# Cross attention in a decoder layer: exponentials of two head groups added on VectorE, masked weights on GpSimd, scans moved

## The chip, the cores and the metric

The kernel runs on one core of a Trainium2 chip. The metric is the device time of one execution in microseconds (us). A core has engines that each work through their own queue of instructions in order: TensorE (PE, matrix products; PEld is its weight load), VectorE (DVE), ScalarE (ACT), GpSimd (POOL) and SyncE (SP, which issues most DMAs). Engines wait for one another through semaphores. SBUF is the working memory of 128 partitions; PSUM is the memory that TensorE writes to, and GpSimd does not read it here.

## The reference

Three blocks on x of shape (4, 512, 512): causal self attention, causal cross attention over a context, and a feed-forward block with two experts' weights. All are float32. The cross attention, cut to what matters:

```python
def _mha(q, k, v):                       # q = layernorm(x), k = v = ctx; 16 heads of 32
    scores = jnp.einsum('bhqd,bhkd->bhqk', qh, kh) / math.sqrt(hd)
    causal = ki <= qi
    scores = jnp.where(causal[None, None], scores, -10000.0)
    attn = jax.nn.softmax(scores, axis=-1)
    return jnp.einsum('bhqk,bhkd->bhqd', attn, vh)

x = x + self_attention(layernorm(x))     # causal, mask of -inf, with projections
x = x + _mha(layernorm(x), ctx, ctx)
x = x + feed_forward(layernorm(x))
```

The mask of the cross attention is -10000 and not minus infinity, so a row whose largest score lies very low would give weight to the keys behind it as well. The kernel computes that weight: for each query the sum of the later context rows ("behind", a running sum from the end) and their number, both times exp(-10000 - maximum).

## The kernel before

The four batches run one after the other in the loop at L845. Each passes through these stages: maxima of the self scores (`with_maxima` L781, filled up with projection matmuls of other blocks), self attention (`attend` L811), output projection (L632), maxima of the cross scores, cross attention, transposes and layernorm (`add_cross` L662), and the feed-forward matmuls, most of which are used as filler in later maxima stages. The order on PE, DVE, ACT and POOL is written out by hand (`manual_schedule`, L836): an engine's queue holds its instructions in the order in which the Python code issues them. Buffers and PSUM come from pools. PSUM has four pairs of banks (`pair`, L65); a new pair waits for the readers of the one that it replaces.

Heads go in four groups g of four heads (128 partitions). The keys go in four blocks of 128; the attention works in units (g, (0,)), (g, (1,)) and (g, (2, 3)). For one unit, `scores` (L360) multiplies keys and queries for four heads and adds minus the row maximum, in two PSUM pairs of two heads each; ScalarE takes the exponential (L402) and GpSimd clears what lies above the diagonal (`affine_select`, L404). Two units later `values` (L416) multiplies the exponentials with the values and, in a second set of matmuls with a matrix of ones, adds them up for the denominators (the loop over u, L425). After a group's last unit `divide` (L493) adds the masked weights, inverts the denominators through two 32x32 block transposes (`inverse`, L481) and multiplies.

In the self attention groups 0 to 2 are "added" (L265): the ones matmuls are left out; instead `add_up` (L453) adds the exponentials of the later units onto the first unit's tile on VectorE, and one set of four matmuls with ones (`summed`, L462) is done on the sum while the next group runs. In the cross attention no group is added.

In the cross attention `behind` (L618) computes the running sum of a group of context columns on VectorE, called in `attend` at L829 after the scores of the group's first unit. `masked` (L348), called after the scores of the group's last unit, spreads the row maxima with one matmul, takes the exponential on ScalarE (L353), and makes two products with `min` on VectorE (L356 and L357), for the numerator and for the denominator.

`with_maxima` also takes a list `norms` of small jobs, one of which it puts behind every second unit's reductions; the cross call at L863 gives none. In `out_projection` the matmuls of L638 come first, with transposes of the context as side work, and then the additions to x and the layernorm.

Of the kernel before, what the change touches and what calls it, by code (L numbers as in the profile page):

```python
# [9 lines left out]
F32 = mybir.dt.float32  # L10
# [16 lines left out]
def decoder_layer(  # L27
# [232 lines left out]
    class Attention:  # L260
        def __init__(self, q_t, k_t, v, cross, name):
            self.q_t, self.k_t, self.v, self.cross, self.name = q_t, k_t, v, cross, name
            self.nm, self.mrow, self.pv, self.out = {}, {}, {}, None
            self.more, self.sums, self.rden, self.e = {}, {}, {}, None
            self.added = () if cross else range(NC - 1)  # L265

        def maxima(self, g, blocks):

# [79 lines left out]
        def masked(self, g):  # L348

            bc = pair(f"mb_{self.name}_{g}")  # L350
            nc.tensor.matmul(bc[:, 0, :], lhsT=same, rhs=self.mrow[g], start=True, stop=True)
            count = work.tile([P, S], F32, tag="count", name=f"ct_{self.name}_{g}")
            nc.scalar.activation(count, bc[:, 0, :], AF.Exp, bias=mbias)  # L353

            beh = self.e.beh_t[:, g, :]
            nc.vector.scalar_tensor_tensor(beh, count, 1.0, beh, ALU.min, ALU.mult)  # L356
            nc.vector.scalar_tensor_tensor(count, count, 1.0, cnt, ALU.min, ALU.mult)  # L357
            self.more[g] = (beh, count)

        def scores(self, g, blocks):  # L360


            at = {j: sum(S - k * P for k in blocks if k < j) for j in blocks}
            N = sum(S - j * P for j in blocks)
            name = f"{self.name}_{g}_{blocks[0]}"
            scs = [pair(f"sc_{name}_{n}") for n in range(2)]
            for j in blocks:
                for r in range(HG):
                    h = slice(r * HD, (r + 1) * HD)
                    nc.tensor.matmul(  # L370
                        scs[r // 2][:, r % 2, at[j] : at[j] + S - j * P],
                        lhsT=self.k_t[h, g, j * P : (j + 1) * P],
                        rhs=self.q_t[h, g, j * P :],
                        start=(j == blocks[0]),
                        stop=False,
                        skip_group_check=(len(blocks) > 1),
                    )
# [12 lines left out]
            if blocks[0] == 0 and g in self.added:  # L390

                self.sums[g] = act.tile(
                    [P, 2, 2, S], F32, tag=("ck_t", "beh_t")[g % 2], name=f"sum_{name}"
                )
            for n in range(2):

                W = N if len(blocks) == 1 else S
                if blocks[0] == 0 and g in self.added:
                    pt = self.sums[g][:, n]
                else:  # L400
                    pt = work.tile([P, 2, W], F32, tag=f"pt{blocks[0]}", name=f"pt_{name}_{n}")
# [12 lines left out]
            return pts  # L414

        def values(self, g, blocks, pts):  # L416

            first, last = blocks[0] == 0, blocks[-1] == NT - 1  # L420
            if first:
                self.pv[g] = pair(f"pv_{self.name}_{g}")
            pv = self.pv[g]
            at = {j: sum(S - k * P for k in blocks if k < j) for j in blocks}
            for u in range(1 if g in self.added else 2):  # L425
                for j in blocks:
                    for r in range(HG):
                        h = g * HG + r
                        nc.tensor.matmul(  # L429
                            pv[r * HD : (r + 1) * HD, u, j * P :],  # L430
                            lhsT=ones if u else self.v[:, j, h * HD : (h + 1) * HD],
                            rhs=pts[r // 2][:, r % 2, at[j] : at[j] + S - j * P],
                            start=(j == 0),
                            stop=(j == NT - 1),
                        )
            if first and g == 0 and not self.cross:
                self.out = act.tile([P, NC, S], F32, tag="o_t", name=f"oT_{self.name}")
            if first and g - 1 in self.added:
                self.sum_in = pv if g in self.added else pair(f"ls_{self.name}")
                self.summed(g - 1, self.sum_in)  # L440
            if first and g - 2 in self.added:
                self.scale(g - 2)
            if blocks == (1,) and g - 1 in self.added and g not in self.added:
                self.spread(g - 1, self.sum_in)
                self.scale(g - 1)
            if last and g in self.added:
                nc.scalar.copy(self.out[:, g, :], pv[:, 0, :])
                if g > 0:
                    self.spread(g - 1, pv)
            elif last:  # L450
                self.divide(g)
# [38 lines left out]
            )  # L490
            return den_t

        def divide(self, g):  # L493
            pv = self.pv.pop(g)
            num, den = pv[:, 0, :], pv[:, 1, :]
            if self.cross:
                beh, count = self.more.pop(g)
                nc.vector.tensor_tensor(count, den, count, ALU.add)
                nc.vector.tensor_tensor(beh, num, beh, ALU.add)
                num, den = beh, count  # L500
                self.out = self.e.beh_t
            rden = self.inverse(g, den)
            nc.vector.tensor_tensor(self.out[:, g, :], num, rden, ALU.mult)
# [128 lines left out]
    def out_projection(e, a, sides):  # L632

        b = e.b
        pms = [pair(f"pm_o{b}_{n}") for n in range(2)]
        for c in range(NC):
            for t in range(NT):
                nc.tensor.matmul(  # L638
                    pms[t // 2][:, t % 2, :],
                    lhsT=a.out[:, c, t * P : (t + 1) * P],  # L640
                    rhs=wo_sb[:, c, :],
                    start=(c == 0),
                    stop=(c == NC - 1),
                )
            if c < NC - 1:
                run(sides[c::3])

        def add(t):
            xi = e.x[:, t, :]
            nc.vector.tensor_tensor(xi, pms[t // 2][:, t % 2, :], xi, ALU.add)  # L650

        made, norms = layernorms(lambda t: e.x[:, t, :], f"q{b}", add)
        run(norms)
        return made
# [156 lines left out]
    def attend(a, late):  # L811

        units = [(g, j) for g in range(NC) for j in ((0,), (1,), (2, 3))]
        waiting = []

        def values():
            g, j, pts = waiting.pop(0)
            a.values(g, j, pts)
            if g in a.added and j != (2, 3):
                a.add_up(*waiting[0])  # L820

        for n, (g, j) in enumerate(units):
            waiting.append((g, j, a.scores(g, j)))
            if n == 4:
                for copy in a.rows(late):
                    copy(nc.scalar.copy)
            if len(waiting) > 2:
                values()
            if a.cross and j == (0,):  # L829
                behind(a.e, g)  # L830
            if a.cross and j == (2, 3):
                a.masked(g)
        while waiting:
            values()

    with tc.manual_schedule(engines=BY_HAND):  # L836
# [8 lines left out]
        for b in range(B):  # L845
# [14 lines left out]
            norm_cross(e, made)  # L860
            ca = Attention(e.cq_t, e.ck_t, e.cv, True, f"c{b}")
            ca.e = e
            late = with_maxima(steps[3:], ca)  # L863
            if b + 2 < B:
                after.x = load_x(b + 1)
            attend(ca, late)
# [70 lines left out]
```

## Time and profile before

| | |
|---|---|
| median of 3 runs | 830.17 us (830.14 to 830.20) |
| profiled execution | 829.93 us |
| its span (first to last instruction) | 828.2 us |
| granted TensorE clock | 0.999 |
| PE / DVE / ACT / POOL busy in the span | 813.8 / 547.0 / 397.9 / 297.8 us |
| output projection, batch 1 | 287.8 to 314 us |
| maxima of the cross scores, batch 1 | 318 to 367 us |
| first cross value matmul to next projection, batch 1 | 367.06 to 397.43 us |
| the same in batches 0, 2 and 3 | 163.81, 557.0 and 732.0 us on |

How to read it: the page gives the busy time of each engine, its share of the span and the number of instructions. The chain that ended last is followed back from the last instruction, at each step to what released it, and its shares say which engine's work set the end. A timeline row is start, duration, engine, source line, operation, output<-inputs, the size of the tile and the number of instructions merged; idle time in front of it stands in brackets with what ended it. In a row of groups the two numbers after the bar are the total busy time and the mean ns of one instruction. A windows row is a stretch with its length and the busy time of PE, PEld, DVE, ACT and POOL in it, and the count of instructions in brackets.

Some durations of single instructions of before that the working uses, from the groups: L356 694 ns, L357 706 ns, L623 (the scan) 1227 ns, L498 692 ns, L499 681 ns, L484 702 ns, L486 254 ns, L487 712 ns, L503 794 ns, L402 814 ns (768 wide) and 1021 ns (1024 wide), L539 (GpSimd, two inputs, 512 wide) 1270 ns. In the timelines a GpSimd select of 256 takes 0.41 us and of 512 0.64 us where nothing holds it up; VectorE's additions of 512 and 256 take 0.68 and 0.51 us.

### The profile page before, as it was taken

To read this page: it belongs to the slowest core of one execution; us is meant where nothing else is said; L and a number is where in the kernel's file an instruction comes from. 1 tells how busy PE (TensorE), PEld (TensorE's weight loads), DVE (VectorE), ACT (ScalarE), POOL (GpSimd) and SP (SyncE) were. 2 spreads that over 40 slices of the span, in tenths; PEclk is the share of its full clock that TensorE was granted. 3 is DMA by queue.
4 is the path that set the end of the run, shared out by engine and by line. 5 is a ranking of instruction groups with operands and counts; after the bars stand their busy time and mean duration, and the time that the engine had idled before them with its cause. 6 is when DMAs were issued, how large, how long until landed. Compare 5 with 4: busy or idle time off the path is not lost.

```text
span 828.2 us, 14453 instructions
## 1 busy us (share of the span) xinstructions
PE 813.8 (98%) x5800; PEld 369.4 (45%) x5800; DVE 547.0 (66%) x937; ACT 397.9 (48%) x502; POOL 297.8 (36%) x549
## 2 busy tenths in 40 slices
PE   9999999999999999999999999999998999999998
PEld 7344444345444454334534444434543444444443
DVE  2578736877678834687858863687779835887511
ACT  2456526761546515556054651676166714574110
POOL 4434512442334732234233471244233643333100
PEclk9999999999999999999999999999999999999999
DMA  9600000001010000030100000000102000000101
GB/s 340 232 27 15 1 1 1 2 2 51 5 35 13 2 1 1 0 103 2 51 14 13 2 2 0 1 2 2 53 16 72 18 1 0 1 2 2 51 0 51
DMA packets 13539, 24.54 MB, mean 30 GB/s; under 512 B 1952, under 2 KB 1952, under 8 KB 13472
## 3 DMA queue, kind: packets, MB, share of 16 engines
q1 hardware_dynamic: 13184, 23.09, 8.2%
q8 instruction: 45, 0.74, 0.4%
q10 hardware_dynamic: 288, 0.52, 0.2%
q14 instruction: 22, 0.18, 0.1%
HBM read 19.42 MB, written 4.19 MB: 29 GB/s over the span
## 4 chain that ended last, share of the span: by engine, by line
PE 92%; ACT 3%; DVE 3%; issue 2%; DMA 0%; POOL 0%; ACTq 0%
PE pm_qk L233 12%; PE pv_c L429 9%; PE pm_u L233 7%; PE pm_d L221 7%; PE pm_v L221 7%; PE pm_o L638 7%; PE pm_e L221 6%; PE pv_s L429 6%; PE sm_c L280 6%; PE sc_s L370 5%; PE sc_c L370 5%; PE sm_s L280 5%; PE sc_s L381 1%; DVE nm_s L310 1%; PE sc_c L381 1%
## 5 line engine op out<-in xcount | busy, mean ns | idle before, releaser
L310 DVE TENSOR_REDUCE nm_c<-s_c 128x2 f32<-128x256 f32 (+3 forms) x128 | 96.3, 810 | 36.6 <-POOL s_c L298 36.6
L310 DVE TENSOR_REDUCE nm_s<-s_s 128x2 f32<-128x256 f32 (+3 forms) x128 | 96.6, 810 | 28.1 <-POOL s_s L298 28.1
L292 ACT COPY s_s<-sm_s 128x768 f32<-128x768 f32 (+1 forms) x96 | 78.9, 874 | 67.2 <-PE sm_s L280 50.9
L292 ACT COPY s_c<-sm_c 128x768 f32<-128x768 f32 (+1 forms) x96 | 78.9, 875 | 48.8 <-PE sm_c L280 34.5
L402 ACT ACTIVATE pt_c<-sc_c 128x768 f32<-128x768 f32 (+1 forms) x96 | 78.6, 883 | 28.7 <-PE sc_c L381 24.8
L298 POOL TENSOR_SCALAR_AFFINE_SELECT s_c<-s_c 128x256 f32<-128x256 f32 (+1 forms) x96 | 46.7, 487 | 119.1 <-ACT s_c L292 118.1
L404 POOL TENSOR_SCALAR_AFFINE_SELECT pt_c<-pt_c 128x256 f32<-128x256 f32 (+1 forms) x96 | 56.7, 598 | 71.0 <-ACT pt_c L402 70.1
L298 POOL TENSOR_SCALAR_AFFINE_SELECT s_s<-s_s 128x256 f32<-128x256 f32 (+1 forms) x96 | 46.9, 491 | 96.7 <-ACT s_s L292 95.7
L458 DVE TENSOR_TENSOR sum_s<-sum_s,pt_s 128x512 f32<-128x512 f32 (+1 forms) x72 | 63.2, 915 | 7.4 <-PE pv_s L429 6.4
L221 PE MATMUL pm_d<-wdown_sb,hT 128*128 128x512 f32 x128 | 60.4, 607 | 0.0
L402 ACT ACTIVATE pt_s<-sc_s 128x768 f32<-128x768 f32 (+1 forms) x72 | 55.9, 838 | 8.9 <-PE sc_s L381 6.4
L221 PE MATMUL pm_e<-wexp_sb,fT 128*128 128x512 f32 x128 | 60.2, 605 | 0.0
L233 PE MATMUL pm_u<-fT,wup_sb 128*128 128x512 f32 x128 | 59.9, 608 | 0.0
L370 PE MATMUL sc_s<-qT,kT 32*128 32x128 f32 (+3 forms) x512 | 58.2, 467 | 0.9 <-ACT sum_s L402 0.9
L233 PE MATMUL pm_qk<-xnT,wk_sb 128*128 128x512 f32 x120 | 58.6, 610 | 0.0
L638 PE MATMUL pm_o<-wo_sb,oT_s 128*128 128x512 f32 x128 | 57.8, 596 | 0.0
L221 PE MATMUL pm_v<-wv_sb,xnT 128*128 128x512 f32 x128 | 57.6, 598 | 0.0
L233 PE MATMUL pm_qk<-xnT,wq_sb 128*128 128x512 f32 x120 | 57.4, 604 | 0.0
L404 POOL TENSOR_SCALAR_AFFINE_SELECT pt_s<-pt_s 128x256 f32<-128x256 f32 (+1 forms) x72 | 48.7, 681 | 21.0 <-ACT pt_s L402 19.8
L370 PE MATMUL sc_c<-cqT,ckT 32*128 32x128 f32 (+3 forms) x512 | 51.8, 467 | 0.9 <-ACT pt_c L402 0.9
L280 PE MATMUL sm_c<-ckT,cqT 32*128 32x512 f32 (+3 forms) x512 | 49.1, 467 | 1.2 <-ACT cqT L257 1.2
L280 PE MATMUL sm_s<-kT,qT 32*128 32x512 f32 (+3 forms) x512 | 48.1, 467 | 0.0
(148 smaller groups left out, 1186.2 us busy)
## 6 DMA issues: line engine op xcount, KB each, us to landing
cv<-in_ctx_dram SPq DMA_DIRECT2D x16, 256.0 KB, 4.1
out_dram<-x SPq DMA_DIRECT2D x16, 256.0 KB, 2.0
x<-in_x_dram SPq DMA_DIRECT2D x14, 256.0 KB, 4.7
xin<-in_x_dram SPq DMA_DIRECT2D x12, 256.0 KB, 2.7
wq_sb<-in_wq_dram SPq DMA_DIRECT2D x2, 512.0 KB, 6.0
wk_sb<-in_wk_dram SPq DMA_DIRECT2D x2, 512.0 KB, 7.7
wv_sb<-in_wv_dram SPq DMA_DIRECT2D x1, 1024.0 KB, 8.3
wo_sb<-in_wo_dram SPq DMA_DIRECT2D x1, 1024.0 KB, 9.9
```

What stands on the lines that cost most here:

```text
L221: nc.tensor.matmul(pm, lhsT=lhs_t[:, c, t * P : (t + 1) * P], rhs=w[:, c, :], start=(c == 0), stop=(c == NC - 1),)
L233: nc.tensor.matmul(pm, lhsT=w[:, c, f * P : (f + 1) * P], rhs=rhs_t[:, c, :], start=(c == 0), stop=(c == NC - 1),)
L280: nc.tensor.matmul(scs[r // 2][:, r % 2, at[i] : at[i] + (i + 1) * P], lhsT=self.q_t[h, g, i * P : (i + 1) * P], rhs=self.k_t[h, g, : (i + ...
L292: nc.scalar.copy(s[:, :, :N], scs[n][:, :, :N])
L298: nc.gpsimd.affine_select(out=diagonal, in_=diagonal, compare_op=ALU.is_ge, fill=NEG, base=0, pattern=[[0, 2 * len(blocks)], [-1, P]], cha ...
L310: nc.vector.tensor_reduce(self.nm[g][:, i, 2 * n : 2 * n + 2], made[n][:, :, at[i] : at[i] + (i + 1) * P], axis=AX.X, op=ALU.max, negate=True,
L370: nc.tensor.matmul(scs[r // 2][:, r % 2, at[j] : at[j] + S - j * P], lhsT=self.k_t[h, g, j * P : (j + 1) * P], rhs=self.q_t[h, g, j * P :] ...
L402: nc.scalar.activation(pt[:, :, :N], scs[n][:, :, :N], AF.Exp)
L404: nc.gpsimd.affine_select(out=diagonal, in_=diagonal, compare_op=ALU.is_ge, fill=0.0, base=0, pattern=[[0, 2 * len(blocks)], [1, P]], chan ...
L429: nc.tensor.matmul(pv[r * HD : (r + 1) * HD, u, j * P :], lhsT=ones if u else self.v[:, j, h * HD : (h + 1) * HD], rhs=pts[r // 2][:, r % ...
L458: nc.vector.tensor_tensor(to, to, pts[n][:, :, at[j] : at[j] + S - j * P], ALU.add)
L638: nc.tensor.matmul(pms[t // 2][:, t % 2, :], lhsT=a.out[:, c, t * P : (t + 1) * P], rhs=wo_sb[:, c, :], start=(c == 0), stop=(c == NC - 1),)
```

## The change

Groups 0 and 2 of the cross attention are added: VectorE adds their exponentials into one tile, which lies in the buffer of the self values (tag `v`), and four matmuls with ones sum it during the next group, in a PSUM pair of its own (`ls`). The division of such a group comes after the next group's second unit; its numerator is taken out of PSUM right after its last unit (`gather`). The two products of `masked` go to GpSimd and lose their `min`; the last column, which has no key behind it, is set to zero by a memset instead. The scans of groups 0 and 1 go into the output projection, in front of the additions to x, and those of groups 2 and 3 between the maxima, behind the reductions of units (0, (0, 1)) and (0, (3,)).

```diff
-            self.added = () if cross else range(NC - 1)
+            self.added = (0, 2) if cross else range(NC - 1)
...
-            nc.scalar.activation(count, bc[:, 0, :], AF.Exp, bias=mbias)
-
+            nc.scalar.activation(count[:, : S - 1], bc[:, 0, : S - 1], AF.Exp, bias=mbias)
+            nc.gpsimd.memset(count[:, S - 1 :], 0.0)
             beh = self.e.beh_t[:, g, :]
-            nc.vector.scalar_tensor_tensor(beh, count, 1.0, beh, ALU.min, ALU.mult)
-            nc.vector.scalar_tensor_tensor(count, count, 1.0, cnt, ALU.min, ALU.mult)
+            nc.gpsimd.tensor_tensor(beh, count, beh, ALU.mult)
+            nc.gpsimd.tensor_tensor(count, count, cnt, ALU.mult)
...
-                self.sums[g] = act.tile(
-                    [P, 2, 2, S], F32, tag=("ck_t", "beh_t")[g % 2], name=f"sum_{name}"
-                )
+                tag = "v" if self.cross else ("ck_t", "beh_t")[g % 2]
+                self.sums[g] = act.tile([P, 2, 2, S], F32, tag=tag, name=f"sum_{name}")
...
-            if first and g - 2 in self.added:
+            if first and g - 2 in self.added and not self.cross:
                 self.scale(g - 2)
             if blocks == (1,) and g - 1 in self.added and g not in self.added:
-                self.spread(g - 1, self.sum_in)
-                self.scale(g - 1)
-            if last and g in self.added:
+                if self.cross:
+                    self.divide(g - 1, self.sum_in[:, 1, :])
+                else:
+                    self.spread(g - 1, self.sum_in)
+                    self.scale(g - 1)
+            if last and g in self.added and self.cross:
+                self.gather(g)
+            elif last and g in self.added:
...
+        def gather(self, g):
+
+            num = self.pv.pop(g)[:, 0, :]
+            beh = self.more[g][0]
+            nc.vector.tensor_tensor(beh, num, beh, ALU.add)
+
+        def divide(self, g, den=None):
+            if den is None:
+                pv = self.pv[g]
+                num, den = pv[:, 0, :], pv[:, 1, :]
             if self.cross:
-                beh, count = self.more.pop(g)
+                num, count = self.more[g]
                 nc.vector.tensor_tensor(count, den, count, ALU.add)
-                nc.vector.tensor_tensor(beh, num, beh, ALU.add)
-                num, den = beh, count
+                if g not in self.added:
+                    self.gather(g)
+                den = count
                 self.out = self.e.beh_t
...
             if c < NC - 1:
                 run(sides[c::3])
+        for g in (0, 1):
+            behind(e, g)
...
-            if a.cross and j == (0,):
-                behind(a.e, g)
...
-            late = with_maxima(steps[3:], ca)
+            scans = [(lambda g=g: behind(e, g)) for g in (2, 3)]
+            late = with_maxima(steps[3:], ca, norms=scans)
```

More of the change, by code (lines that the diff above doesn't have):

```diff
@@ L491, in inverse @@
             return den_t
-        def divide(self, g):
-            pv = self.pv.pop(g)
-            num, den = pv[:, 0, :], pv[:, 1, :]
+        def gather(self, g):
[6 more added lines that the diff above has]
+                num, den = pv[:, 0, :], pv[:, 1, :]
             if self.cross:
-                beh, count = self.more.pop(g)
+                num, count = self.more[g]
                 nc.vector.tensor_tensor(count, den, count, ALU.add)
-                nc.vector.tensor_tensor(beh, num, beh, ALU.add)
-                num, den = beh, count
+                if g not in self.added:
+                    self.gather(g)
+                den = count
                 self.out = self.e.beh_t
```

## The prediction

> **What bounds the kernel now.** Read first: the page's busy shares and its chain, then the cross-attention stage of batch 1 by itself, then the timeline inside it, then the self-attention stage of the same batch, which already adds up exponentials on VectorE.
>
> ```profile
> PE 813.8 (98%) x5800; PEld 369.4 (45%) x5800; DVE 547.0 (66%) x937; ACT 397.9 (48%) x502; POOL 297.8 (36%) x549
> PE 92%; ACT 3%; DVE 3%; issue 2%; DMA 0%; POOL 0%; ACTq 0%
> ...
> 367.06:397.43 30.37, 30.37 (x413) 12.74 (x409) 23.69 (x36) 19.86 (x26) 12.97 (x25) 1.00 0.11 36
> ```
>
> TensorE is busy all the time and is 92% of the chain; in the cross stage (last line: first value matmul to the next projection) it never idles. So work taken off TensorE there is worth its full time, until another engine's result comes too late. The other engines have room: VectorE 6.7 of 30.37, GpSimd 17.4.
>
> ```profile
> 367.06 1.06 PE L429 MATMUL pv_c<-pt_c,cv 128*32 128x512 f32 x8
> 367.94 1.04 PE L429 MATMUL pv_c<-pt_c,ones 128*32 128x512 f32 x8
> 368.92 0.39 PE L351 MATMUL mb_c<-mrow_c,same 128*128 128x512 bf16 x1
> 370.52 0.85 PE L429 MATMUL pv_c<-pt_c,cv 128*32 128x384 f32 x8
> 371.95 0.93 PE L370 MATMUL sc_c<-cqT,ckT 32*128 32x384 f32 x8
> 373.30 0.86 PE L429 MATMUL pv_c<-pt_c,cv 128*32 128x256 f32 x16
> 374.74 0.94 PE L370 MATMUL sc_c<-cqT,ckT 32*128 32x256 f32 x16
> ...
> 261.10 1.06 PE L429 MATMUL pv_s<-sum_s,v 128*32 128x512 f32 x8
> 262.10 1.22 PE L370 MATMUL sc_s<-qT,kT 32*128 32x512 f32 x8
> 263.47 0.85 PE L429 MATMUL pv_s<-pt_s,v 128*32 128x384 f32 x8
> 264.25 1.22 PE L370 MATMUL sc_s<-qT,kT 32*128 32x384 f32 x8
> 265.89 0.86 PE L429 MATMUL pv_s<-pt_s,v 128*32 128x256 f32 x16
> 266.68 1.12 PE L370 MATMUL sc_s<-qT,kT 32*128 32x256 f32 x12
> 284.20 1.04 PE L464 MATMUL ls_s<-sum_s,ones 128*32 128x512 f32 x8
> 285.06 0.83 PE L429 MATMUL pv_s<-pt_s,v 128*32 128x384 f32 x8
> ```
>
> Starts are the clean measure. With the ones matmuls (cross) the three value units of a group take 368.92-367.06 = 1.86, 1.43 and 1.44; without them (self) 1.00, 0.78 and 0.79. The summing matmuls take 0.86.
>
> ```profile
> 277.59 1.98 POOL L479 TENSOR_TENSOR oT_s<-oT_s,dt_s 128x512 f32<-128x512 f32 x1
> 278.36 2.03 DVE L458 TENSOR_TENSOR sum_s<-sum_s,pt_s 128x768 f32<-128x768 f32 x1
> 284.84 1.28 POOL L479 TENSOR_TENSOR oT_s<-oT_s,dt_s 128x512 f32<-128x512 f32 x1
> ```
>
> These decide the forecast. GpSimd's product takes 1.28 alone. Started at 277.59, while VectorE was in the addition before, it lasted to 279.57; the next addition, begun at 278.36, ended at 280.39, only 0.82 behind it. The two do not share: an addition of two SBUF tensors and a GpSimd product run one after the other, and each holds the other up for its full length.
>
> **The change part by part.** The sum goes against the profiled execution's 829.93 (span 828.2 and 1.7 around it); the median of the runs is 830.17, 0.03% above.
>
> *Ones matmuls, groups 0 and 2.* Gone 0.86 + 0.65 + 0.65 = 2.16 a group, added 0.86 for the summing matmuls: -1.30 a group, eight groups, -10.4 on the path.
>
> *Score units that now come early.* TensorE reaches a score unit sooner, but its second pair of heads needs a PSUM pair that ScalarE's exponentials free; those take 1.94 a unit of four 512-wide heads and 1.51 otherwise, as before. The self stage shows it: its score unit at 264.25 is followed by the next step (265.57) after 1.32, the cross unit at 371.95 after 1.02. In the changed program's order the summing result takes a PSUM pair too (`ls`), so that scores (2,0) wait for VectorE's denominator addition (0.69). Taken: 0.33 + 0.31 + 0.11 + 0.40 in group 0's round, 0.37 for `ls`, 0.31 + 0.31 + 0.09 in group 2's: 2.23 a batch, +8.9. Bounds: 1.5 a batch (self loses 0.8 in its first round and 0.37 in each of two more) and 3.2 (eight waits of the largest, 0.4).
>
> *VectorE.* An added group gets six additions, 2 x (0.82 + 0.68 + 0.51) = 4.0 (the six of L458 in self took 4.99 to 5.99 with GpSimd beside them); every group loses two masked products (0.69 + 0.69, L356 and L357) and a scan (1.22). The gather addition of an added group waits for GpSimd's product and for the last value matmul; behind it in VectorE's queue stand only divisions, but the summing matmuls wait for it. In the stage: +8.0 - 5.5 - 4.9, so its load hardly moves, but the additions stand behind the division of the group before, which takes 3.8 (0.69, 0.68, 0.70, 0.25, 0.71, 0.70 and gaps).
>
> *GpSimd.* Each group gets a memset (0.10) and two products of 1.28 on top of its selects (four of 0.41, two of 0.64 alone): 2.9 becomes 5.6. In its queue the products stand between the selects of unit (g,(2,3)) and those of (g+1,(0)), which TensorE's value matmuls wait for. Bounds of a product: 1.28 alone, 1.98 beside an addition; I take 1.28 and put the waits in separately.
>
> A page speaks against this part. The Trainium skill, GPSIMD Engine Reference, section 3.1 Elementwise, gives 4497 ns for a 2048-wide two-input addition, about twice VectorE's. Scaled to 512 that is an estimate of 1.12; the trace's 1.28 decides, and by the page's figure the time would come out 2.6 lower (0.16 x 4 x 4: of a batch's eight products about four stand in the way).
>
> *The turns, batch 1, from the rows above* (us from the stage's first value matmul; unit (g,j) is head group and key block):
>
> ```
> TensorE reaches     before  after   what held it in between
> values (0,0)          0.00   0.00
> values (1,0)          8.71   8.31   banks; 0.60 for the select of (1,0), behind both products
> summing group 0         -   10.60   0.55 for the gather addition behind the six additions
> values (1,1)         12.17  13.54   0.37, ls bank
> values (2,0)         17.09  18.46
> values (2,1)         20.55  21.37   0.31
> values (3,0)         25.46  26.96   0.31, 0.21; 1.45 for the second select of (3,0)
> summing group 2         -   30.11   1.40 for the gather addition
> next projection      30.37  34.27
> ```
>
> Group 0's round: the products can start at 2.55, after the spread maxima's exponential; with the first two additions between them they end at 6.59, the selects of (1,0) at 7.55 and 8.40 (TensorE wants the second at 7.86), the additions, one select after each, at 9.91 and gather at 10.53 (TensorE is there at 10.05). The worst place, group 2: the division of group 1 ends at 21.59. Then in turns: product 22.86, addition 23.69, product 24.88, addition 25.71, select 26.04, addition 26.70, select 27.05 (the one awaited, TensorE was there at 25.51), addition 27.55, select 27.90, addition 28.56, select 28.91, addition 29.41, gather 30.04 (TensorE was there at 28.70). TensorE's lost turns are 0.60 + 0.55 + 1.45 + 1.40 + 0.1 = 4.1 a batch. Behind it comes group 3's division, which waits for GpSimd's last product and ends 0.1 after the transposes want it.
>
> With the first two parts: -2.6 + 2.2 + 4.1 = +3.7, and 0.1 at the transposes. In batch 3 VectorE enters the stage with its splits still to do (the last rows seen, 733.88 on, against a stage start of 732.0), 0.5 more. Four batches: 3.83 x 4 + 0.5 = +15.8.
>
> *Scans.* Each takes its memset (0.10) along in GpSimd's queue, between selects that have gaps of over 1; no DMA moves. Two go in front of the additions of the output projection. VectorE idles 13.2 there waiting for L638 (11.4 in batch 3), and the context columns are in SBUF by then: 0. Two go between the maxima. In batches 0 and 2 VectorE has gaps of only 0.60, 0.53, 0.60, 0.39 and 0.20 there, 2.3 against 2 x 1.22; the row copy of group 0 would end at 143.0 instead of 142.2, and the maxima matmuls that need its bank start at 143.45. I take 0; the bounds are 0 and 4 x 2.44 = +9.8 if none of it hid.
>
> *The rest.* The sum tile lies where the self values were, last read at 287.8 and written again only by the cross exponentials after 360: no wait. The divisions of groups 0 and 2 come earlier: 0, nothing reads them before the transposes; group 3's stays under the filler projection of 3.63.
>
> Sum: 829.93 - 10.4 + 8.9 + 16.9 (4.1 x 4 and 0.5) + 0.4 = 845.7; forecast **845.5**.
>
> **The rivals.**
> *A, the matmuls come off and nothing is late:* -10.4, 819.5. For it: the self stage adds up three groups at 7.17 a group (268.12 to 275.29) and only small bank waits. Against: there GpSimd does one product a group, off the path of the selects, and no division stands before the additions. It ends on the other side; it decides where the select of (3,0) and the gather of group 2 are both ready before 25.5 and 28.7.
> *B, GpSimd and VectorE do not hold each other up:* the bank waits alone, -10.4 + 8.9 = -1.5, 828.4. Against it: the three rows above.
> *C, products near 1.98 throughout:* by the same count 0.7 x 4 x 4 = 11 more, 857.
> *D, the scans in the maxima push TensorE:* up to 9.8 more, 855. Batches 1 and 3 speak against it: VectorE idles 2 to 3.7 at a time there.
>
> **How the numbers follow.** What a measurement can tell from no change is taken as 0.2%, 1.7. Chances: forecast 0.73 (own range 838 to 850), A 0.04, B 0.07 (0.04 of it within 0.2%), C 0.08, D 0.08. Faster 0.07, same 0.04, slower 0.89. The range leaves out A, B's better half and the ends of C and D: 834 to 854; its low end is where half of the turns' waits are hidden and the bank waits are at their lower bound.
>
> **What would show it.** TensorE in a cross stage about 34 from its first value matmul to the next projection, with idle before pv_c and ls_c put down to GpSimd's select and VectorE's additions; products of 1.3 to 2.0; additions stretched over 0.82; the maxima and output projection stages unchanged in length. Wrong if the second select of (3,0) ends before TensorE arrives, if products and additions overlap at their lone lengths, or if the score units lose less than the self stage's 0.3 each.

## The result, and the profile after

The changed kernel takes 837.98 us (median, 837.95 to 838.03). Against the kernel before the ratio is 1.0096, 95% interval 1.0082 to 1.0109: slower by 7.8 us. The prediction was 845.5 with a range of 834 to 854. Direction and mechanism came out as forecast; the sum was 7.5 too high.

First the page of the changed kernel: the busy times, the chain, and the group of the additions in cross attention.

```profile
PE 815.7 (98%) x5608; PEld 369.7 (44%) x5608; DVE 582.5 (70%) x953; ACT 398.0 (48%) x502; POOL 350.9 (42%) x597
...
PE 86%; DVE 6%; issue 4%; ACT 3%; DMA 0%; POOL 0%; DVEq 0%
...
L463 DVE TENSOR_TENSOR sum_c<-sum_c,pt_c 128x768 f32<-128x768 f32 (+2 forms) x48 | 53.4, 1150 | 3.4 <-PE pv_c L429 2.9
```

TensorE has 192 instructions fewer and is busy 1.9 longer: matmuls that wait for a PSUM pair start further apart but still overlap, so the wait counts as busy time and not as idle time. VectorE is now 6% of the chain. Then the four cross stages as windows:

```profile
163.94:196.08 32.14, 30.89 (x365) 13.13 (x361) 25.16 (x30) 19.85 (x26) 24.98 (x34) 1.00 0.01 2
369.15:401.06 31.91, 30.65 (x365) 13.24 (x361) 26.72 (x36) 19.95 (x26) 25.23 (x34) 1.00 0.11 35
560.77:592.91 32.14, 30.89 (x364) 13.13 (x361) 25.16 (x30) 19.85 (x26) 24.98 (x34) 1.00 0.01 2
737.75:769.98 32.23, 30.97 (x364) 13.05 (x361) 27.05 (x36) 20.04 (x26) 25.48 (x34) 1.00 0.00 1
```

Each stage took 30.37 before, so they lose 1.77 + 1.54 + 1.77 + 1.86 = 6.9 of the 8.0 by which the span grew (836.2 against 828.2). The transposes behind the stage are the other place (199.62 to 201.59, 1.97 instead of 1.74; four times, 0.9). The maxima and the output projection keep their lengths.

The timeline of batch 1 around group 2 shows the turns, and what TensorE waits for.

```profile
388.17 1.53 PE L371 MATMUL sc_c<-cqT,ckT 32*128 32x512 f32 x8
...
389.35 1.55 POOL L357 TENSOR_TENSOR behT<-ct_c,behT 128x512 f32<-128x512 f32 x1
389.68 2.02 DVE L463 TENSOR_TENSOR sum_c<-sum_c,pt_c 128x768 f32<-128x768 f32 x1
...
390.97 1.87 POOL L358 TENSOR_TENSOR ct_c<-ct_c,cnt 128x512 f32<-128x512 f32 x1
391.63 2.02 DVE L463 TENSOR_TENSOR sum_c<-sum_c,pt_c 128x768 f32<-128x768 f32 x1
392.79 1.13 POOL L404 TENSOR_SCALAR_AFFINE_SELECT pt_c<-pt_c 128x256 f32<-128x256 f32 x1
...
393.58 0.88 DVE L463 TENSOR_TENSOR sum_c<-sum_c,pt_c 128x512 f32<-128x512 f32 x1
...
393.88 0.85 POOL L404 TENSOR_SCALAR_AFFINE_SELECT pt_c<-pt_c 128x256 f32<-128x256 f32 x1
...
394.67 0.25 PEld L429 LDWEIGHTS pv_c<-pt_c,cv 128*32 128x32 f32 x8 [1.14 <-POOL pt_c L404]
...
394.70 1.13 PE L429 MATMUL pv_c<-pt_c,cv 128*32 128x512 f32 x8 [0.94 <-ACT pt_c L402]
...
396.28 0.68 DVE L502 TENSOR_TENSOR behT<-pv_c,behT 128x512 f32<-128x512 f32 x1
...
397.01 1.07 PE L469 MATMUL ls_c<-sum_c,ones 128*32 128x512 f32 x8 [0.32 <-DVE behT L502]
```

Read the ends. Product 390.90, addition 391.70, product 392.84, addition 393.65, select 393.92, addition 394.46, select 394.73: the two engines alternate, with not one end out of turn. TensorE stands for 0.94 before the values of (3,0) until the second of these selects is done (the weight load's row names GpSimd; the matmul's row names ScalarE, which had long been done), and for 0.32 before the summing until gather is done. The first row is the other cost: eight score matmuls took 1.53, where the same row lasts 1.14 in the kernel before (at 369.24). Here are the groups of these matmuls, of the kernel before and of the changed one, and ScalarE's row beside the score unit at 388.17:

```profile
L370 PE MATMUL sc_c<-cqT,ckT 32*128 32x512 f32 x128 | 18.2, 640 | 0.0
...
L371 PE MATMUL sc_c<-cqT,ckT 32*128 32x512 f32 x128 | 24.3, 640 | 0.0
...
387.00 1.51 ACT L402 ACTIVATE pt_c<-sc_c 128x768 f32<-128x768 f32 x2 [0.96 <-PE sc_c L382]
```

A single matmul lasts 640 ns on average in both, but together the 128 cover 24.3 instead of 18.2. In the unit at 388.17 the second pair of heads starts at 388.57, 0.40 behind the first pair (0.01 in the kernel before), just after ScalarE's exponentials of the unit before end at 388.51.

### The profile page after: what moved, and what is told of

It reads as the page before. It is cut to its first block, busy times and chain, and to the rows that moved or that the text cites. A ratio compares the mean times of both kernels' runs of the same rounds, so it can differ in the third digit from the quotient of the medians.

```text
span 836.2 us, 14133 instructions
## 1 busy us (share of the span) xinstructions
PE 815.7 (98%) x5608; PEld 369.7 (44%) x5608; DVE 582.5 (70%) x953; ACT 398.0 (48%) x502; POOL 350.9 (42%) x597
## 4 chain that ended last, share of the span: by engine, by line
PE 86%; DVE 6%; issue 4%; ACT 3%; DMA 0%; POOL 0%; DVEq 0%
PE pm_qk L233 12%; PE pm_u L233 7%; PE pm_d L221 7%; PE pm_v L221 7%; PE pm_o L651 7%; PE pm_e L221 6%; PE pv_s L429 6%; PE sm_c L280 6%; PE sc_s L371 5%; PE sm_s L280 4%; PE pv_c L429 4%; PE sc_c L371 4%; DVE sum_c L463 2%; PE sc_s L382 1%; DVE nm_s L310 1%
## 5 line engine op out<-in xcount | busy, mean ns | idle before, releaser
L298 POOL TENSOR_SCALAR_AFFINE_SELECT s_c<-s_c 128x256 f32<-128x256 f32 (+1 forms) x96 | 48.7, 509 | 116.7 <-ACT s_c L292 115.7
L402 ACT ACTIVATE pt_c<-sc_c 128x768 f32<-128x768 f32 (+1 forms) x80 | 64.7, 857 | 26.0 <-PE sc_c L382 18.8
L371 PE MATMUL sc_c<-cqT,ckT 32*128 32x128 f32 (+3 forms) x512 | 61.2, 467 | 0.9 <-ACT sum_c L402 0.9
L404 POOL TENSOR_SCALAR_AFFINE_SELECT pt_c<-pt_c 128x256 f32<-128x256 f32 (+1 forms) x80 | 51.5, 662 | 15.7 <-ACT pt_c L402 14.8
L463 DVE TENSOR_TENSOR sum_c<-sum_c,pt_c 128x768 f32<-128x768 f32 (+2 forms) x48 | 53.4, 1150 | 3.4 <-PE pv_c L429 2.9
```

The lines of the kernel that those rows point to most:

```text
L298: nc.gpsimd.affine_select(out=diagonal, in_=diagonal, compare_op=ALU.is_ge, fill=NEG, base=0, pattern=[[0, 2 * len(blocks)], [-1, P]], cha ...
L371: nc.tensor.matmul(scs[r // 2][:, r % 2, at[j] : at[j] + S - j * P], lhsT=self.k_t[h, g, j * P : (j + 1) * P], rhs=self.q_t[h, g, j * P :] ...
L404: nc.gpsimd.affine_select(out=diagonal, in_=diagonal, compare_op=ALU.is_ge, fill=0.0, base=0, pattern=[[0, 2 * len(blocks)], [1, P]], chan ...
L463: nc.vector.tensor_tensor(to, to, pts[n][:, :, at[j] : at[j] + S - j * P], ALU.add)
```

## The experiments

| run | us | ratio to before, 95% interval | stage, batch 1 |
|---|---|---|---|
| scans_only | 829.93 | 1.0000 (0.9991 to 1.0008) | 30.37 |
| products_gpsimd_no_adds | 830.07 | 1.0001 (0.9992 to 1.0010) | 30.36 |
| adds_products_out | 828.97 | 0.9988 (0.9979 to 0.9997) | 30.13 |
| adds_products_dve | 838.73 | 1.0105 (1.0089 to 1.0120) | 31.08 |
| products_later | 837.93 | 1.0097 (1.0083 to 1.0111) | 32.11 |
| own_pair | 837.99 | 1.0097 (1.0083 to 1.0111) | 31.92 |
| gather_later | 836.80 | 1.0082 (1.0067 to 1.0096) | 31.61 |
| gather_later_mb_in_pair | 836.63 | 1.0080 (1.0067 to 1.0093) | 31.60 |
| group0_mb_in_pair | 833.94 | 1.0047 (1.0033 to 1.0061) | 31.17 |
| blocks_joined_dve | 837.08 | 1.0086 (1.0072 to 1.0099) | 31.81 |
| blocks_joined_gpsimd | 837.63 | 1.0093 (1.0079 to 1.0107) | 32.88 |
| half_groups_dve | 841.76 | 1.0142 (1.0128 to 1.0156) | 33.30 |

The theory: an added group gives 1.30 of matmuls and loses it to score units that wait for PSUM pairs; what makes the kernel slower is that GpSimd's products and VectorE's additions take turns. The rivals are in the expectations. A diff is against the changed kernel.

**Scans alone.**

```diff
-            self.added = (0, 2) if cross else range(NC - 1)
+            self.added = () if cross else range(NC - 1)
...
-            nc.gpsimd.tensor_tensor(beh, count, beh, ALU.mult)
-            nc.gpsimd.tensor_tensor(count, count, cnt, ALU.mult)
+            nc.vector.scalar_tensor_tensor(beh, count, 1.0, beh, ALU.min, ALU.mult)
+            nc.vector.scalar_tensor_tensor(count, count, 1.0, cnt, ALU.min, ALU.mult)
...
```

> Only the scans are moved; the masked products are VectorE's again and no exponentials are added up in cross attention. Theory (the scans are hidden in their new places, as the prediction's zero for them says): the time of before, 830.2 within 0.8. Rival (the 1.05 us that the changed kernel loses outside its four cross stages, 8.0 of its span against 6.95 in the stages, come from the scans): 831.2. Second rival (the scans were a load that VectorE felt in the cross stages): below 829.4.

829.93, stages of 30.37: the scans cost nothing and give nothing.

**Products on GpSimd without additions.**

```diff
-            self.added = (0, 2) if cross else range(NC - 1)
+            self.added = () if cross else range(NC - 1)
```

> Scans moved and masked products on GpSimd, but no exponentials added up. Theory (products harm only where additions take turns with them): every product 1.28 except beside one of VectorE's additions of two SBUF tensors, selects ready long before TensorE wants them, cross stages 30.4, time 830.2 within 0.8. Rival (2.6 us of products in front of the selects are late by themselves): idle of TensorE before pv_c put down to a select, 1 a group in the worst places, up to 846.

830.07. The numerator's products of this run, all 16 (min/median/max in ns):

```profile
L357 POOL TENSOR_TENSOR behT<-ct_c,behT x16: 1273/1277/1281, 166.8 to 760.5; 128x512 f32<-128x512 f32 x16
```

and of the changed kernel:

```profile
L357 POOL TENSOR_TENSOR behT<-ct_c,behT x16: 1267/1415/2101, 167.1 to 768.2; 128x512 f32<-128x512 f32 x16
```

Without additions beside them the products never vary; with them they reach 2.10. So neither the scans nor the products do harm alone.

**Additions, products left out.**

```diff
-            nc.gpsimd.tensor_tensor(beh, count, beh, ALU.mult)
-            nc.gpsimd.tensor_tensor(count, count, cnt, ALU.mult)
```

> As the changed kernel, but both products of the masked weights are left out (the divisions read the unmasked weights and sums). It prices the turns by themselves. Theory: additions at their lone lengths, no wait for a select or for gather, the bank waits stay: 832.0 within 1, cross stages 30.4. Rival (bank waits are small and it is the turns that cost all): 837.98 - 8.0 - 10.4 + 8.9, that is below 829. Rival (turns do not matter): 837 to 838.

828.97: 9.0 less than the changed kernel, a little below the kernel before (the interval ends at 0.9997). The theory's 832.0 was 3.0 too high: it had counted 1.5 a batch from two idle rows, and the products cost 2.0 in the stage (1.8 in batch 1) and 0.23 at the transposes. The first rival's figure (below 829) came out with half of its reason: the products cost more than all that the kernel lost, but the bank waits are not small, as shown next. VectorE in batch 1, groups 0 and 2, six additions in a row each, and the window of the stage:

```profile
368.91 4.42 DVE L461 TENSOR_TENSOR sum_c<-sum_c,pt_c 128x768 f32<-128x768 f32 x6
...
386.85 4.51 DVE L461 TENSOR_TENSOR sum_c<-sum_c,pt_c 128x768 f32<-128x768 f32 x6
...
366.50:396.63 30.13, 30.13 (x364) 12.82 (x360) 21.49 (x36) 19.64 (x26) 11.95 (x26) 1.00 0.12 36
```

In the changed kernel the same rows are 6.47 and 6.67. Here TensorE has no idle time in the stage (PE busy 30.13 of 30.13), and yet the stage is only 0.24 shorter than before, although 2.60 of matmuls are gone. The difference, 2.36 a batch, is the waits of the score units: 7.63 - (8.71 - 2.16) = 1.08 up to the values of (1,0), then 0.65 at the score unit behind the summing, 0.40 up to values (2,1) and 0.25 up to values (3,0). So the additions gain about 0.24 a batch in this order when no product is in their way.

**Products on VectorE.**

```diff
-            nc.gpsimd.tensor_tensor(beh, count, beh, ALU.mult)
-            nc.gpsimd.tensor_tensor(count, count, cnt, ALU.mult)
+            nc.vector.scalar_tensor_tensor(beh, count, 1.0, beh, ALU.min, ALU.mult)
+            nc.vector.scalar_tensor_tensor(count, count, 1.0, cnt, ALU.min, ALU.mult)
...
```

> As the changed kernel, but the masked products on VectorE as before. Theory: the waits of 1.06 for the second select of (3,0) and of 0.46 for the gather addition of group 2 (batch 1 of the changed kernel) come from products and additions taking turns; without them VectorE needs 1.65 + 1.4 + 1.65 + 0.7 = 5.4 behind the division of group 1 that ends at 20.6, so gather is done at 26.0 when TensorE is there at 26.3. The bank waits of 2.4 a batch stay. 838.0 - 4 x 1.5 = 832.0, cross stages 30.4. Rival (the additions alone make VectorE late, wherever the products are): 836 to 838 or more, idle of TensorE before ls_c put down to VectorE.

838.73; the theory's 832.0 was wrong. The rival's time is right and its reason is not: the additions alone cost nothing in the run without products. Additions and products together are too much for VectorE's queue. The select of (3,0) is no longer late, but VectorE is, in two places. Timeline of batch 1:

```profile
391.48 0.88 DVE L356 SCALAR_TENSOR_TENSOR behT<-ct_c,behT 128x512 f32<-128x512 f32 x1
...
393.10 2.49 DVE L462 TENSOR_TENSOR sum_c<-sum_c,pt_c 128x512 f32<-128x512 f32 x4
395.50 0.68 DVE L501 TENSOR_TENSOR behT<-pv_c,behT 128x512 f32<-128x512 f32 x1
...
396.24 1.06 PE L468 MATMUL ls_c<-sum_c,ones 128*32 128x512 f32 x8 [0.56 <-DVE behT L501]
...
398.39 0.69 DVE L356 SCALAR_TENSOR_TENSOR behT<-ct_c,behT 128x512 f32<-128x512 f32 x1 [2.20 <-ACT ct_c L354]
...
406.55 0.66 PE L681 MATMUL tp_x<-ident,behT 128*128 128x128 f32 x4 [1.25 <-DVE behT L515]
```

The four short additions took 2.49 where 1.65 was counted. By their lone lengths (0.68 and 0.51) they need 2.38, so most of this was a miscount. The two products before them took 1.62 and not 1.4, because the selects take turns with these as well (0.88 in the first row, 0.69 alone). So gather ends 27.0 after the stage's start, not 26.0. And group 3's products wait for ScalarE in front of the division of group 2 and that of group 3 in the same queue, so the transposes wait 1.25 in every batch. Stages 0.71 to 0.78 longer and transposes 1.47 longer (198.44 to 201.65 in batch 0, 1.74 before), four times, are 8.8 of the 8.9 that the span grew. Against the run without products they cost 9.8 on VectorE and 9.0 on GpSimd.

**Products later in GpSimd's queue.**

```diff
-            if a.cross and j == (2, 3):
-                a.masked(g)
+            if a.cross and j == (0,) and g > 0:
+                a.masked(g - 1)
+        if a.cross:
+            a.masked(NC - 1)
```

> As the changed kernel, but the masked weights of a group are worked out after the score unit (g+1,0) instead of before it, so that on GpSimd the products stand behind the selects that TensorE waits for. Theory: the wait of 1.06 for the second select of (3,0) goes; the products then take turns with later additions, so the gather addition stays late by 0.5 and the end of the stage, where the products of group 3 come later, loses up to 1: 834 to 838. Rival (the queue place does not matter, all additions and products are one sequence whose sum decides): 838 or above.

837.93. The wait table of TensorE (total us, times, longest) in the changed kernel:

```profile
PE pv_c L429 <- ACT pt_c L402: 3.7, 4, 0.9
...
PE ls_c L469 <- DVE behT L502: 1.3, 4, 0.3
```

and with the products later:

```profile
PE ls_c L469 <- DVE behT L502: 4.5, 4, 1.1
...
PE sc_c L371 <- DVE behT L502: 0.9, 4, 0.2
```

The wait for the select is gone, and the waits for gather have grown by as much: 5.0 in all in the changed kernel, 5.4 here. So here one sequence of turns decides, and its order only says which wait ends it. The time lies where the two forecasts meet (up to 838, and from 838); the waits decide for the rival.

**The sum in the group's own PSUM pair.**

```diff
-                self.sum_in = pv if g in self.added else pair(f"ls_{self.name}")
+                if self.cross:
+                    self.sum_in = self.pv[g - 1]
+                else:
+                    self.sum_in = pv if g in self.added else pair(f"ls_{self.name}")
...
-            num = self.pv.pop(g)[:, 0, :]
+            num = self.pv[g][:, 0, :]
```

> As the changed kernel, but the summing result of an added group goes into the free half of the group's own PSUM pair, so that no pair is taken for it and the summing matmuls wait for the additions alone, not for the gather addition (0.68 behind them). Theory: the 0.46 before the summing of group 2 and the 0.07 before that of group 0 go, and no more; 838.0 - 4 x 0.5 = 836.0. Rival (the pair taken for the sum is what costs the bank waits around it, 0.63 at the score unit behind group 0's): 833.5. Rival (the pair is held longer and the waits only move): 838.

837.99: nothing. The edit did not take the wait away; the summing matmuls still show 1.3 in four waits for gather:

```profile
PE pv_c L472 <- DVE behT L505: 1.3, 4, 0.3
```

They now write to the pair whose other half gather reads. So the next run issues gather later:

```diff
+                if self.cross:
+                    self.sum_in = self.pv[g - 1]
...
             if last and g in self.added and self.cross:
-                self.gather(g)
+                pass
...
-                if g not in self.added:
-                    self.gather(g)
+                self.gather(g)
```

> As the changed kernel, but the summing result goes into the free half of the group's own PSUM pair, and the gather addition of an added group is issued behind the denominator's addition. Where the run own_pair left the summing matmuls waiting for gather (0.32 before them, released by VectorE's addition into behT), they now wait for the additions of the exponentials alone, which end 0.6 earlier. Theory: 0.46 + 0.07 a batch go, 838.0 - 2.1 = 835.9. Rival (the numerators' pair is then freed 0.7 later, and a score unit that takes it waits as long): 838.

836.80, 1.2 gained where 2.1 was expected. Summing follows the values of (1,0) after 1.74 and those of (3,0) after 1.71 (1.91 and 2.31 in the changed kernel), so the waits are gone. But from the summing of group 0 to the values of (1,1) it takes 3.63 instead of 3.25: the pair is held longer, and about half is given back. Both the theory and the rival were half right.

**The spread maxima in the pair too, and group 0 alone.**

```diff
-            bc = pair(f"mb_{self.name}_{g}")
+            if g in self.added:
+                bc = self.pv[g][:, 1:2, :]
+            else:
+                bc = pair(f"mb_{self.name}_{g}")
...
```

> As gather_later, and the spread maxima of an added group (one matmul of 512) go into the free half of the group's PSUM pair too, so that in these rounds one PSUM pair fewer is taken in turn by the score units. Theory (the score units wait for pairs): about 0.3 of the 1.07 in group 0's round and 0.3 in group 2's go, 2.4 in all: 833.5. Rival (they wait for ScalarE's pace and not for the number of pairs): as gather_later.

836.63, as gather_later. In group 0's round TensorE reaches the values of (1,0) at 7.34 instead of 7.62, so that wait was for a pair; but it reaches those of (1,1) at 12.98, as it did without (12.99). With `self.added = (0,)` besides:

> As gather_later_mb_in_pair, but only group 0 is added up; group 2 has its ones matmuls back. It parts the two groups. Theory: group 0's round gives 1.30 a batch and loses about 1.3 in bank waits, nothing waits for a select or for additions, and the stage's end is that of before: 830.0 within 1. Rival (an added group costs as much wherever it stands, half of the changed kernel's 7.9): 832 to 834.

833.94, +4.0 against before: half of the changed kernel's loss, which is the rival's number. Its reason does not hold: the run above, which differs by group 2 alone, takes 836.63, so group 2 costs 2.7 there and group 0 costs 4.0. The timeline of batch 1, where nothing is added up beside the score unit (2,0), says why:

```profile
378.79 0.69 DVE L516 TENSOR_TENSOR ct_c<-pv_c,ct_c 128x512 f32<-128x512 f32 x1 [1.89 <-PE pv_c L475]
379.00 0.69 ACT L357 ACTIVATE ct_c<-mb_c,mbias 128x511 f32<-128x511 f32 x1 [1.17 <-PE mb_c L354]
...
379.74 0.19 PEld L374 LDWEIGHTS sc_c<-cqT,ckT 32*128 32x128 f32 x2 [0.55 <-ACT ct_c L357]
```

Two pairs hold values and denominators of groups 0 and 1, one the first two heads of the new scores; the other two heads need the pair of the spread maxima, and wait until ScalarE has read it. From the maxima's matmul (378.58) to the values of (1,1) (381.02) it takes 2.44, before 1.60: 0.84 lost. Another 0.48 goes between the values of (1,0) and the maxima: TensorE is there earlier, at 375.38, and the last two heads start at 375.83, when their select ends (375.82). With 0.79 up to there (7.34 against 6.55) group 0 loses 2.1 and gives 1.30.

**The work split in other ways.** Each group's block 1 is added onto block 0, and one ones matmul goes over both (cut to its core):

```diff
+        def join(self, g, blocks, pts):
+            for n in range(2):
+                to = self.sums[g][n][:, :, P:]
+                nc.vector.tensor_tensor(to, to, pts[n][:, :, : S - P], ALU.add)
...
+                if u and g in self.joined:
+                    if first:
+                        continue
+                    if blocks == (1,):
+                        for r in range(HG):
+                            nc.tensor.matmul(pv[r * HD : (r + 1) * HD, 1, :], lhsT=ones,
+                                rhs=self.sums[g][r // 2][:, r % 2, :], start=True, stop=False)
+                        continue
```

> Another split of the same work: in every group the exponentials of key block 1 are added onto those of block 0 (two additions of 768 a group in place of twelve for two groups), and one ones matmul goes over both, without summing matmuls and without a further PSUM pair; masked products on VectorE, a division's last four steps behind the additions in VectorE's queue, scans as in the changed kernel. It takes 0.65 a group from TensorE, 16 groups, -10.5. Theory (a score unit loses 0.33 only where the value unit before it has no ones matmuls, here once a group): + 16 x 0.35 = 5.6, and 0.5 a batch where VectorE enters the stage late: 827. Rival (VectorE's queue, 0.69 x 2 + 1.6 + 2.4 + 1.4 = 6.8 of the 7.7 a group, makes additions late by 0.5 a group and more): 833 or above.

> As the run before it, with the masked products on GpSimd. Theory (products and additions take turns): the two additions of a group and its two products together take 2 x 0.82 + 2 x 1.28 = 4.2 in place of 1.64, so the ones matmul over both blocks or the selects of the next group come late by 0.3 to 0.8 a group: 829 to 838. Rival (two additions are few enough to pass): as the run before it, 827 or below.

837.08 and 837.63: the rival's range in the first, the theory's in the second. Batch 1 of the first:

```profile
378.89 1.53 PE L372 MATMUL sc_c<-cqT,ckT 32*128 32x512 f32 x8
379.86 0.78 PE L383 MATMUL sc_c<-mrow_c,onesb 32*128 32x512 bf16 x4
380.57 0.85 PE L447 MATMUL pv_c<-pt_c,cv 128*32 128x384 f32 x8
...
396.72 1.05 PE L436 MATMUL pv_c<-pt_c,ones 128*32 128x512 f32 x4 [0.36 <-DVE pt_c L488]
```

A group's round takes 8.31 where it took 8.38, with 0.65 of matmuls gone. The score unit (2,0) lasts from 378.89 to 380.57, 1.68 against 1.29 before: a value unit without ones matmuls costs the next score unit 0.39. The ones matmul over both blocks takes 1.15 up to the next scores, some 0.2 more than alone. And the last round, with no score units in it, takes 6.1 instead of 4.9, because the additions are late there (last row). With the products on GpSimd the stages of batches 0 and 2 stay at 31.44, and those of 1 and 3, which VectorE enters late, grow by 1.1.

The other split keeps TensorE's load even: in groups 0 to 2 two heads are added up, the other two keep their ones matmuls (cut to its core).

```diff
-                    for r in range(HG):
+                    for r in range(2 if u and g in self.halved else 0, HG):
...
+                if g in self.halved:
+                    for r in range(2):
+                        nc.tensor.matmul(pv[r * HD : (r + 1) * HD, 1, :], lhsT=ones,
+                            rhs=self.sums[g][:, r, :], start=True, stop=True)
...
-            for n in range(2):
+            for n in range(1 if self.cross else 2):
```

> The same kind of work spread evenly: in groups 0, 1 and 2 the exponentials of the first two heads are added up on VectorE (three additions a group), and the other two heads keep their ones matmuls; two summing matmuls at the end of each such group go into its own denominators. Masked products on VectorE, the division's last four steps behind the first addition, scans as in the changed kernel. It takes 0.71 a group from TensorE, 12 groups, -8.5. Theory (a score unit waits only as far as the value unit before it is shorter than ScalarE needs; half of the ones matmuls stay, so 0.1 to 0.2 twice a group): + 3.6, 825. Rival (bank waits take it all, as with joined blocks): 830. Second rival (VectorE late, 6.8 of work in a round of 7.7): 832 or above.

841.76, the slowest of all, and for a reason that no expectation had. Batch 1:

```profile
370.88 1.03 PE L436 MATMUL pv_c<-pt_c,ones 128*32 128x512 f32 x4
371.84 0.39 PE L353 MATMUL mb_c<-mrow_c,same 128*128 128x512 bf16 x1
...
376.91 0.39 PE L436 MATMUL pv_c<-pt_c,ones 128*32 128x256 f32 x2
376.93 0.62 PE L465 MATMUL pv_c<-sum_c,ones 128*32 128x512 f32 x2
...
377.91 0.94 PE L372 MATMUL sc_c<-cqT,ckT 32*128 32x256 f32 x16
...
386.65 1.05 PE L465 MATMUL pv_c<-sum_c,ones 128*32 128x512 f32 x4 [0.29 <-DVE sum_c L479]
```

The ones matmuls of two heads take 0.96 from start to next start; those of four heads took 0.98 (the rows at 367.94 and 368.92 shown of before). So nothing came off TensorE, and the summing matmuls were added. In group 0 they run beside the ones matmuls of the other two heads, and the step from these to the next scores takes 1.00 (376.91 to 377.91) instead of 0.76. In groups 1 and 2 they wait for VectorE (last row) until the others are done, and the same step takes 2.09 and 2.10. Together that is 2.9 a batch, the whole loss. No run beat the kernel before, but for the one that leaves the products out.

## Why the prediction was right, and where its sizes were off

*Ones matmuls, -10.4: right.* The first value unit takes 1.00 and the next two turns shrink as counted; the runs that sum up differ from before by this and the waits alone.

*Bank waits, +8.9: right.* Without products the stages are 0.24, 0.24, 0.25 and 0.17 shorter, 0.9 together, so the waits are 10.4 - 0.9 = 9.5. By place, in batch 1: group 0's round 1.08 (1.15 forecast), behind the summing 0.65 (0.37), group 2's round 0.65 (0.71). The wait behind the summing is the one that the prediction named, but larger: the weights of the last two heads are loaded at 380.66, just after VectorE's addition of the denominators ends at 380.60.

```profile
380.66 0.19 PEld L371 LDWEIGHTS sc_c<-cqT,ckT 32*128 32x128 f32 x2 [0.34 <-DVE ct_c L510]
```

Where `ls` is gone (gather_later, group0_mb_in_pair) the same heads wait 0.55 for ScalarE's reading of the spread maxima instead. Whether more than four pairs would take these waits away, no run shows.

*Turns of products and additions, +16.9, and +0.4 at the transposes: the term that was too large.* The products cost 9.0 in all (837.98 - 828.97). The alternation is there, end by end in the order that the prediction wrote down for group 2; what failed is the step "each holds the other up for its full length". A product behind an addition takes 1.14 of its 1.28, an addition of 512 behind a select 0.54 (392.79 + 1.13 to 393.58 + 0.88) of its 0.68, and a select behind an addition 0.27 of 0.41: 0.14 of each overlaps the other engine's instruction. An addition of 768 behind a product takes 0.80 and 0.81, as forecast, but alone it takes 0.95 (first line, from the run without products); the prediction's 0.82 was read from end to end, and its other lengths were lone ones. The profile of before shows a product's turn as well: the addition in front of the product at 277.59 ended at 278.44 (second line), and the product 1.13 behind it, at 279.57.

```profile
368.91 0.95 DVE L461 TENSOR_TENSOR sum_c<-sum_c,pt_c 128x768 f32<-128x768 f32 x1
...
277.11 1.33 DVE L458 TENSOR_TENSOR sum_s<-sum_s,pt_s 128x768 f32<-128x768 f32 x1
```

From the end of group 1's division to gather's end the prediction counted 8.45; it took 7.20 (389.76 to 396.96).

| wait, batch 1 | forecast | measured |
|---|---|---|
| values (1,0), select, and summing group 0 | 0.60 + 0.55 | 0.18 together |
| values (3,0), second select | 1.45 | 1.01 |
| summing group 2 | 1.40 | 0.57 |
| transposes | 0.1 | 0.23 |

The measured column is the changed kernel against the run without products, start to start, so it holds small waits that no row names. A wait is the difference of two long sums, so 15% of the one (8.45 to 7.20) made nearly half of the other (1.45 + 1.40 to 1.58). The working also disagrees with itself a little: its table of turns has 0.83 of bank waits in group 2's round (0.31, 0.31 and 0.21) and ends 3.9 above before, while its sum takes 0.71 and 3.7. That is 0.7 over four batches.

*Scans, 0: right.* scans_only gives 0 within 0.1%, which also ends rival D. *Rival A* falls with the bank waits, 9.5. *Rival B* is what the run without products makes real: 828.97 against its 828.4. *Rival C:* the median products of 1.42 lie nearer to 1.28 than to 1.98.

*The estimate from the Trainium skill* (GPSIMD Engine Reference, section 3.1), 1.12 for a product alone: the runs have 1.277, so the row of before was the better price.

*What would show it:* products of 1.27 to 2.10, stretched additions and unchanged other stages did appear. The stage was 31.9 to 32.2, not 34, and one of the two waits is named only in the weight load's row.

## What to carry to other kernels

Before work is taken off a busy TensorE, ask what its length was hiding: here 2.36 of 2.60 a batch came straight back as waits for PSUM pairs, and the run that leaves the products out shows how little was left to gain, 0.1%. Where two engines take turns, price a turn from the ends of consecutive rows (0.54, 0.27, 1.14) and not from lone durations, and expect that moving a step within the sequence may move the wait and not the time, as it did here. What an instruction saves is the turn that it frees: two of four matmuls that run side by side free nothing.

## What the runs showed of the hardware

A VectorE addition of two SBUF tensors and a GpSimd instruction on SBUF exclude each other only in their main part: 0.14 of a lone length overlaps the other's instruction (0.23 for an addition of 256, which ended 0.28 behind a select and takes 0.51 alone). Selects are in it as well as products. VectorE's gather, which reads PSUM, is not: it takes 0.68 beside a select of 0.63 to 0.81, as alone. The Trainium skill, SBUF — State Buffer, section "SBUF: two separate sides", says that the shared port pair is held "for the whole instruction" by a VectorE operation with two SBUF inputs or a GpSimd operation. The traces agree on who is in it; on the length they show 1.14 of a product's 1.28 and 0.27 of a select's 0.41.

The ones matmuls of two heads, each 32 columns wide, last as long as those of four, 0.96 against 0.98. The Trainium skill, TensorE: Matmul & The Clock Gate, "Part 3: Packing small matmuls", says that matmuls whose outputs lie on different 32-partition groups run concurrently; the trace agrees, and the half split lost by not reckoning with it.

A wait for a PSUM pair inside a unit lengthens the merged row (1.53 for 1.14) and no single matmul (640 ns on average in both kernels), and in these units it appears as idle time in no row of PE; the weight load's row may show it (0.55 behind ScalarE's L357).
